# Two attention and feed-forward layers on one core: a gated unit's second product as an operation of its own, a scale moved into weights, and a newly drawn instruction order

## The chip, the cores and the metric

The kernel runs on one core of a Trainium2 chip. The metric is the device time of one execution in microseconds (us). PE is the matrix engine (TensorE; PEld is its weight loading), DVE the vector engine, ACT the scalar engine, POOL is GpSimd, and SP the queue that issues most transfers. All data are float32 except where said; a float32 product of a 128 x 512 operand shows in the trace as two matmuls.

## The reference

The input x has 128 sequences of 64 tokens with 128 features, 8192 tokens in all; the context has the same shape. Four steps follow each other, each added to x:

```python
x = x + _L0_xattn_ref(_layernorm(x), ctx, ctx, ...)   # 16 heads of 8, layer norms before and behind, gated
x = x + _L0_ffn_ref(_layernorm(x), ...)
x = x + _L1_xattn_ref(_layernorm(x), ctx, ctx, ...)   # 16 heads of 8
x = x + _L1_ffn_ref(_layernorm(x), ...)               # relu, 128 -> 512 -> 128
```

The change is in the first feed-forward. Its weights hold -1, 0 and 1, and each product is scaled by output feature:

```python
def _tlin(x, w, s):
    return jnp.einsum('bsi,oi->bso', x, w) * s
h = silu(_tlin(x, w1_w, w1_s)) * _tlin(x, w2_w, w2_s)   # 128 -> 512
h = gelu(_tlin(h, h1_w, h1_s))                          # 512 -> 512
h = gelu(_tlin(h, h2_w, h2_s))                          # 512 -> 512
return _tlin(h, w3_w, w3_s)                             # 512 -> 128
```

## The kernel before

**Tiling.** The tokens are cut into 17 chunks: one of 256 tokens, 15 of 512, one of 256 (`GROUPS`, in units of 128). Each chunk goes through four stages, each a Python generator: `attention0`, `ffn0`, `attention1`, `ffn1`. The chunk's x stays in SBUF from its load to its store. PSUM is used as eight banks of 128 x 512; a block of attention scores for four sequences takes four of them.

**The order of the work.** The kernel is written out in a fixed order by a planner that runs while the program is built (`Order`). Generators yield operations (`Op`) that name an engine, a planned length from a table (`LENGTHS`) and the buffers they take (`get`) and give back (`put`): banks, and numbered SBUF buffers such as `wk`, `hd`, `e`, `kx`, `qx`, `x` and `c`. At each step the planner takes, of all streams, the operation that can start first by its own clocks. Ties go by the stream's priority plus a small pseudo-random draw (`draw`), seeded by an entry of `DRAWS` for each 50 us of planned PE time; a seed of 0 gives no draw, and 12 of the 24 seeds are 0. Whatever the planner picks is emitted there and then, so its choice is the order of instructions on every engine. Where two engines may do an operation (`(ACT, DVE)`, `(DVE, POOL)`) the planner also picks the engine. Waits between engines are semaphores that follow from the data, not from the planned times. In the first 95 us of planned time PE's idle time is filled with small products of zeros (L428, 40 at the start, 197 in all).

**An attention stage** (`attend`, twice for a chunk of 512 tokens): scores (PE, L658) into four banks, their maximum (DVE, L662), its split in three bf16 parts ("parts", DVE or POOL, L672 to L675), the transpose of these (PE, L679; copied by ACT, L682), the scores less the maximum (PE, L691, four banks), the exponential (ACT, L696, into `e`), the weighted values (PE, L710), and small steps on ACT, DVE (L720 to L728) and POOL (L742). Layer norms take their moments on DVE (L541, L543), their inverse root on POOL (L529), and the normalising on ACT (L568) or DVE (L572); the norm behind the first attention is L564 and L876 on DVE. Transposes are L582, products for queries, keys and values L606, L618 and L631, token-major products L770.

**The first feed-forward** (`ffn0`). For each quarter k of the 512 hidden features `gated` makes two products of the normalised tokens, L903 into one bank and L904 into another, taken and given out together. ACT takes the tanh of the first (L907), and DVE makes the gated value in two steps: (tanh + 1) times the first product (L909), and that times the scales times the second product (L910). Both banks and the tanh's buffer come free behind L910. Then `square` runs twice: the 512 x 512 product in seven products of halves (PE, L956), with differences of inputs on POOL (L938), sums on DVE (L982), copies on ACT or DVE (L512, L514), and gelu on ACT (L975). At the end the token-major product with `w3` (L770) lands in a bank; DVE multiplies it by the last scale's row into a `wk` buffer (L1046), and POOL adds that to x (L1048). POOL makes the sums of weights for `square` once, early (`weights`, L896).

**Set-up on DVE.** `masks` adds up a table of head masks in five small steps (L479 to L483) and scales four biases with it (L487). `folds` folds the identity matrix into an 8-column selector in four steps (L799 to L804) and spreads it in four copies into `asel` (L808), which the scores less max use.

`ffn1` ends with the add into x (L1103) and the store (L1105). ACT changes between two function tables, one for exp and tanh and one for gelu; a load of one is ACT_TABLE_LOAD.

Of the kernel before, what the change touches and what calls it, by code (L numbers as in the profile page):

```python
# [8 lines left out]
F32 = mybir.dt.float32  # L9
# [5 lines left out]
P = 128  # L15
# [23 lines left out]
for _n, _w in _COLS:  # L39
# [25 lines left out]
DRAWS = [97, 0, 427, 0, 249, 0, 0, 0, 575, 0, 0, 112, 0, 817, 0, 39, 412, 0, 615, 329, 0, 15, 762, 0]  # L65
# [13 lines left out]
        "scores": (0.99, 0.2), "max transpose": (0.07, 0.2), "scores less max": (1.17, 0.2),  # L79
        "weighted values": (0.92, 0.2), "tokens": (0.22, 0.15), "tokens 4": (0.9, 0.15), "w12": (1.73, -0.2),  # L80
# [3 lines left out]
        "bias+": 0.28, "masks": 1.2, "gate weights": 0.4, "folds": 1.9, "moments": 1.07, "z": 1.3, "copied": 0.68,  # L84
        "scaled": 0.75, "qx": 1.5, "kx": 1.5, "vb": 1.8, "max": 2.3, "parts": 0.8, "reciprocal": 2.2, "o2": 0.83,
        "from bank": 0.68, "gate sums": 1.3, "gate": 0.4, "gained": 1.1, "gated": 1.45, "sum": 0.68, "saved": 0.68,
# [236 lines left out]
def kernel(  # L323
# [107 lines left out]
    busy(40, 7)  # L431
    ident = const.tile([P, P], F32, tag="ident", name="ident")
# [3 lines left out]
    half_mask = const.tile([P, 2, 4], F32, tag="half_mask", name="half_mask")  # L436
# [22 lines left out]
    def rowv(name, ng):  # L459
        return each(row[:, ROW[name], :], ng)  # L460
# [42 lines left out]
    fold = const.tile([P, 2, 32], F32, tag="fold", name="fold")  # L503
# [290 lines left out]
    def folds():  # L794

        yield Op(DVE, "folds")

        nc.vector.tensor_copy(identb, ident)
        nc.vector.tensor_tensor(  # L799
            fold, ident[:, 0:64].rearrange("p (r c) -> p r c", r=2), ident[:, 64:128].rearrange("p (r c) -> p r c", r=2), ALU.add  # L800
        )
        nc.vector.tensor_tensor(fold[:, 0, :], fold[:, 0, :], fold[:, 1, :], ALU.add)
        for j in range(1, 3):
            nc.vector.tensor_tensor(  # L804
                fold[:, 0, 0:8], fold[:, 0, 0:8], fold[:, 0, 8 * j : 8 * j + 8], ALU.add
            )
        for s in range(HS):
            nc.vector.tensor_copy(  # L808
                asel[:, s, :].rearrange("p (j k) -> p j k", j=2),
                fold[:, 0, 2 * s : 2 * s + 2].unsqueeze(2).to_broadcast([P, 2, 64]),  # L810
            )
# [71 lines left out]
    def weights(l):  # L883
# [131 lines left out]
    def ffn0(ci, prio):  # L1015
# [3 lines left out]
        fz = Last(fz, 4)  # L1019
# [8 lines left out]
        for l in range(2):  # L1028
# [6 lines left out]
        ps, fp, fw = yield from token_major(  # L1035
# [6 lines left out]
            own=True,  # L1042
# [5 lines left out]
        nc.gpsimd.tensor_tensor(xt, xt, y, ALU.add)  # L1048
# [148 lines left out]
```

## Time and profile before

| | us |
|---|---|
| median of 3 runs | 1130.72 (1130.66 to 1131.59) |
| the profiled execution, whole | 1129.94 |
| its span, first to last instruction | 1128.1 |
| PE busy with matmuls | 1097.8 |
| DVE busy | 865.8 |
| ACT busy | 726.2 |
| POOL busy | 504.5 |

The page gives for each engine its busy time, share of the span and number of instructions. Groups are lines of the kernel with the engine, the tiles written and read, and the mean length of one instruction in ns. A wait is the idle time of an engine ahead of an instruction, put down to the instruction that ended it. Matmul ends are modelled, so PE can be held up a little inside what is shown as busy. The granted clock is the share of its full clock that PE was given.

### The profile page before, as it was taken

The page shows a single profiled execution, that of the slowest core. Times are in us where ns is not written, and L with a number is a line of the kernel's source. Part 1 is how long each engine was busy: PE and PEld are TensorE (multiplying, and loading weights), DVE is VectorE, ACT ScalarE, POOL GpSimd, SP SyncE. Part 2 cuts the span into 40 slices and gives each one's busy share as a digit, 9 for nine tenths or more (in the row PEclk, how much of TensorE's full clock was granted, in tenths as well). Part 3 has the DMA queues.
Part 4 walks back from the last instruction along what each step waited for, and adds up shares of the span by engine and source line. Part 5 has one row for each costly group of instructions (what it writes and reads, how often), then busy time and mean ns, then how long its engine had stood idle before and what let it go on. Part 6 is the DMA issues. An engine that isn't in the chain of part 4 may idle for free.

```text
span 1128.1 us, 32895 instructions
## 1 busy us (share of the span) xinstructions
PE 1097.8 (97%) x13851; PEld 865.0 (77%) x13851; DVE 865.8 (77%) x2139; ACT 726.2 (64%) x1279; POOL 504.5 (45%) x882
## 2 busy tenths in 40 slices
PE   7799999999999999999999999999999999999998
PEld 6578687777876777878677887777778887789786
DVE  7887969888876867568878687788789888643773
ACT  5476767666776766576546686667867675545553
POOL 6744634544533445333226355335345546352221
PEclk9999999999999999999999999999999999999999
DMA  7001000000001001002100000000000000000001
GB/s 244 12 2 30 20 11 20 11 9 17 7 2 35 1 2 39 2 2 57 31 21 20 11 21 11 20 12 12 11 11 12 11 7 11 2 1 2 11 21 43
DMA packets 35444, 23.23 MB, mean 21 GB/s; under 512 B 1504, under 2 KB 34272, under 8 KB 35168
## 3 DMA queue, kind: packets, MB, share of 16 engines
q1 hardware_dynamic: 35024, 21.00, 6.2%
q8 instruction: 109, 1.79, 0.7%
q14 instruction: 39, 0.32, 0.1%
q10 hardware_dynamic: 272, 0.13, 0.0%
HBM read 16.93 MB, written 4.19 MB: 19 GB/s over the span
## 4 chain that ended last, share of the span: by engine, by line
PE 86%; DVE 10%; ACT 2%; issue 1%; POOL 1%; DMA 0%; DVEq 0%; ACTq 0%
PE banks L956 33%; PE banks L770 12%; PE banks L691 7%; PE banks L710 5%; PE banks L658 5%; PE banks L1080 5%; PE banks L903 4%; PE banks L904 4%; PE banks L582 4%; DVE m L662 3%; PE banks L631 2%; PE banks L618 2%; PE banks L606 2%; DVE su L727 1%; DVE st L541 1%
## 5 line engine op out<-in xcount | busy, mean ns | idle before, releaser
L662 DVE TENSOR_REDUCE m<-banks 128x32 f32<-128x2048 f32 x64 | 145.9, 2280 | 16.3 <-PE banks L658 15.7
L742 POOL TENSOR_TENSOR wk<-av,rec 128x256 f32<-128x256 f32 x64 | 46.8, 732 | 222.3 <-DVE rec L728 199.7
L696 ACT ACTIVATE e<-banks 128x2048 f32<-128x2048 f32 x64 | 120.2, 1878 | 36.0 <-PE banks L691 28.8
L956 PE MATMUL banks<-hd,wh 128*128 128x256 f32 (+1 forms) x544 | 127.9, 371 | 0.6 <-DVE wk L909 0.4
L956 PE MATMUL banks<-wk,wh 128*128 128x256 f32 (+1 forms) x544 | 127.5, 371 | 0.0
L956 PE MATMUL banks<-wk,ws 128*128 128x256 f32 (+1 forms) x544 | 126.2, 371 | 0.8 <-POOL wk L938 0.7
L727 DVE RECIPROCAL su<-su 128x256 f32<-128x256 f32 x64 | 111.4, 1741 | 0.0
L956 PEld LDWEIGHTS banks<-wk,wh 128*128 128x128 f32 x544 | 96.4, 190 | 18.0 <-issue 5.7
L975 ACT ACTIVATE hd<-hd,col 128x256 f32<-128x256 f32 (+1 forms) x204 | 88.8, 488 | 31.9 <-DVE hd L982 31.1
L956 PEld LDWEIGHTS banks<-hd,wh 128*128 128x128 f32 x544 | 95.4, 190 | 16.8 <-issue 4.1
L956 PEld LDWEIGHTS banks<-wk,ws 128*128 128x128 f32 x544 | 94.7, 190 | 16.5 <-issue 3.4
L982 DVE TENSOR_TENSOR hd<-banks,hd 128x512 f32<-128x512 f32 (+1 forms) x102 | 66.6, 656 | 53.0 <-PE banks L956 45.4
L529 POOL TENSOR_TENSOR nr<-nv,neg_half 128x4 f32<-128x4 f32 (+1 forms) x102 | 99.7, 977 | 8.5
L938 POOL TENSOR_TENSOR wk<-hd,wk 128x512 f32<-128x512 f32 (+1 forms) x68 | 82.4, 1212 | 40.5 <-DVE hd L910 29.0
L512 ACT COPY hd<-banks 128x512 f32<-128x512 f32 (+1 forms) x68 | 37.9, 557 | 73.0 <-PE banks L956 67.9
L568 ACT ACTIVATE wk<-x,nb,nr 128x128 f32<-128x128 f32 x192 | 79.1, 484 | 7.3 <-POOL nb L559 7.0
L658 PEld LDWEIGHTS banks<-kx,qx 32*128 32x128 f32 x2048 | 62.8, 186 | 22.4 <-issue 10.0
L710 PEld LDWEIGHTS banks<-e,vblk 128*32 128x32 f32 x4096 | 60.2, 110 | 24.0 <-issue 7.6
L658 PE MATMUL banks<-kx,qx 32*128 32x128 f32 x2048 | 74.6, 282 | 2.5 <-ACT qx L597 1.2
L710 PE MATMUL banks<-e,vblk 128*32 128x64 f32 x4096 | 70.4, 220 | 2.2 <-ACT e L696 2.2
L691 PE MATMUL banks<-qx,kx 32*128 32x128 f32 x2048 | 71.5, 277 | 0.0
L903 PE MATMUL banks<-wk,w 128*128 128x512 f32 (+1 forms) x136 | 67.7, 579 | 0.7 <-ACT wk L512 0.7
(136 smaller groups left out, 2367.8 us busy)
## 6 DMA issues: line engine op xcount, KB each, us to landing
c<-in_c_dram SPq DMA_DIRECT2D x30, 256.0 KB, 2.9
x<-in_x_dram SPq DMA_DIRECT2D x15, 256.0 KB, 3.6
out_dram<-x SPq DMA_DIRECT2D x15, 256.0 KB, 2.5
wh<-in_w_h_dram SPq DMA_DIRECT2D x1, 2048.0 KB, 12.5
c<-in_c_dram SPq DMA_DIRECT2D x4, 128.0 KB, 3.2
wa<-in_w_a_dram SPq DMA_DIRECT2D x2, 256.0 KB, 5.1
w<-in_w_dram SPq DMA_DIRECT2D x1, 512.0 KB, 7.7
wf<-in_w_f_dram SPq DMA_DIRECT2D x2, 256.0 KB, 6.9
```

What stands on the lines that cost most here:

```text
L529: nc.gpsimd.tensor_tensor(rs, ve, neg_half[:, 0:ng], ALU.pow)
L658: nc.tensor.matmul(sc[:, g, s, :], qs[h, s, :], ks[h, s, :], start=True, stop=True)
L662: nc.vector.tensor_reduce(m, sc.rearrange("p g s (j k) -> p g (s j) k", j=2), AX.X, ALU.max, negate=True,)
L691: nc.tensor.matmul(sT[:, g, s, :], lhs, rhs, start=(n == 0 and s == 0), stop=(n == 1), skip_group_check=True)
L696: nc.scalar.activation(e.rearrange("p g s i q -> p (g s i q)"), sT.rearrange("p g s c -> p (g s c)"), AF.Exp, scale=SCALE,)
L710: nc.tensor.matmul(po[32 * g : 32 * g + 32, i, s, :], vb[:, 4 * (half * HS + s) + g, i : i + 2].rearrange("p h j d -> p (h j d)"), e[:, g, ...
L727: nc.vector.reciprocal(su, su)
L770: nc.tensor.matmul(ps[:, g, :], lhs(g), w, start=(n == 0), stop=(n == len(blocks) - 1),)
L903: nc.tensor.matmul(pa, w12[:, 0, k * P : (k + 1) * P], zT, start=True, stop=True)
L938: nc.gpsimd.tensor_tensor(T[m][0], x(), y(), ALU.subtract)
L956: nc.tensor.matmul(pieces[bank][0][:, o], w[:, k, o * P : (o + 1) * P], x[:, k], start=(new and k == 0 and o == 0), stop=(k == 1), skip_gr ...
L975: nc.scalar.activation(out(i, t)[:, o], (src or out(i, t))[:, o], AF.Gelu, scale=colv(scale, 2 * i + o))
```

## The change

1. In `gated` the second product becomes an operation of its own in a stream of its own with priority 2. The planner lets it start only behind the planned end of the tanh. It takes its own bank. DVE's two steps become two operations, and the first product's bank comes free behind the first of them.
2. POOL multiplies `w3` by the last scale's row once, behind the second set of weight sums. At the end of `ffn0` DVE adds the product straight into x; the `wk` buffer, the multiplication and POOL's add go.
3. All 24 seeds of `DRAWS` are new and none is 0, so that every stretch is drawn; four planned lengths are changed and the planner's PE clock starts at 2.5 us. With 1, 2 and this, the order of instructions on every engine, and the choice of engine for operations that have two, differs from about the first microsecond on.
4. `masks` and `folds` take fewer and larger DVE steps; the last of the three blank value buffers is cleared only behind the planned landing of the hidden weights.

Cut to its core (line lengths of `DRAWS` shortened by "..."):

```diff
-DRAWS = [97, 0, 427, 0, 249, 0, 0, 0, 575, 0, 0, 112, 0, 817, ...]
+DRAWS = [45944, 71272, 38430, 71272, 71272, 71272, 71272, ...]
...
-"scores less max": (1.17, 0.2), ... "w12": (1.73, -0.2),
+"scores less max": (1.11, 0.2), ... "w12": (0.865, -0.2),
-"masks": 1.2, "folds": 1.9, ... "gated": 1.45,
+"masks": 0.9, "folds": 1.3, ... "gated a": 0.68, "gated b": 0.75,
...
     busy(40, 7)
+    order.clock[PE] = 2.5
...
     def masks():
         yield Op(DVE, "masks")
-        nc.vector.tensor_tensor(half_mask[:, 0, 0:2], hm[:, 0, 0, :], hm[:, 0, 1, :], ALU.add)
-        nc.vector.tensor_tensor(half_mask[:, 1, 0:2], hm[:, 1, 0, :], hm[:, 1, 1, :], ALU.add)
-        nc.vector.tensor_tensor(half_mask[:, 0, 2:4], hm[:, 0, :, 0], hm[:, 0, :, 1], ALU.add)
-        nc.vector.tensor_tensor(half_mask[:, 1, 2:4], hm[:, 1, :, 0], hm[:, 1, :, 1], ALU.add)
-        nc.vector.tensor_tensor(mask, half_mask[:, 0, :], half_mask[:, 1, :], ALU.add)
+        for i, order_of in ((0, "p n s t -> p t n s"), (2, "p n s t -> p s n t")):
+            nc.vector.tensor_reduce(mask[:, i : i + 2], hm.rearrange(order_of), AX.XY, ALU.add)
...
             if i < N_VB:
+                if i == N_VB - 1:
+                    yield Op(NONE, "free", after=landed[7])
                 yield Op(POOL, "blank values", put=[("vb", i)])
...
         nc.vector.tensor_copy(identb, ident)
-        nc.vector.tensor_tensor(fold, ident[:, 0:64]..., ident[:, 64:128]..., ALU.add)
-        nc.vector.tensor_tensor(fold[:, 0, :], fold[:, 0, :], fold[:, 1, :], ALU.add)
-        for j in range(1, 3):
-            nc.vector.tensor_tensor(fold[:, 0, 0:8], fold[:, 0, 0:8], fold[:, 0, 8 * j : 8 * j + 8], ALU.add)
-        for s in range(HS):
-            nc.vector.tensor_copy(asel[:, s, :]..., fold[:, 0, 2 * s : 2 * s + 2]...)
+        rows_of_8 = ident.rearrange("p (r j c) -> p c r j", j=4, c=8)[:, :, :, 0:3]
+        nc.vector.tensor_reduce(fold, rows_of_8, AX.XY, ALU.add)
+        nc.vector.tensor_copy(
+            asel.rearrange("p s (j k) -> p (s j) k", j=2), fold.unsqueeze(2).to_broadcast([P, 2 * HS, SEQ])
+        )
...
     def weights(l):
...
+        if l == 1:
+            yield Op(POOL, "weights")
+            nc.gpsimd.tensor_tensor(w3, w3, rowv("L0_ffn_w3_s", 4), ALU.mult)
...
     def gated(k, zT, n, free, d):
-        pe = yield Op(PE, "w12", get={"bank": 2, "wk": 1}, put=free)
-        pa, pb = (tile_of(s, (P, n)) for s in pe.slots["bank"])
+        got = {}
+
+        def other():
+            pe = yield Op(PE, "w12", get={"bank": 1}, put=free)
+            got["pb"] = (tile_of(pe.slots["bank"][0], (P, n)), pe.slots["bank"])
+            nc.tensor.matmul(got["pb"][0], w12[:, 1, k * P : (k + 1) * P], zT, start=True, stop=True)
+
+        pe = yield Op(PE, "w12", get={"bank": 1, "wk": 1}, put=free)
+        pa = tile_of(pe.slots["bank"][0], (P, n))
         nc.tensor.matmul(pa, w12[:, 0, k * P : (k + 1) * P], zT, start=True, stop=True)
-        nc.tensor.matmul(pb, w12[:, 1, k * P : (k + 1) * P], zT, start=True, stop=True)
         yield Op(ACT, "tanh", prio=-1)
         th = tile_of(pe.slots["wk"][0], (P, n))
         nc.scalar.activation(th, pa, AF.Tanh, scale=half_s1[:, k : k + 1])
-        yield Op(DVE, "gated", put=pe.slots["bank"] + pe.slots["wk"], prio=-1)
+        second = yield (other(), 2)
+        yield Op(DVE, "gated a", put=pe.slots["bank"], prio=-1)
         nc.vector.scalar_tensor_tensor(th, th, 1.0, pa, ALU.add, ALU.mult)
+        yield [second]
+        yield Op(DVE, "gated b", put=got["pb"][1] + pe.slots["wk"], prio=-1)
+        pb = got["pb"][0]
         nc.vector.scalar_tensor_tensor(d[k // 2][0][:, :, k % 2, :], th..., half_s12[:, k : k + 1], pb..., ALU.mult, ALU.mult)
...
     def ffn0(ci, prio):
...
-        fz = Last(fz, 4)
+        fz = Last(fz, 8)
...
-        ps, fp, fw = yield from token_major([...], ng, b[0][1] + b[1][1], own=True)
+        ps, fp = yield from token_major([...], ng, b[0][1] + b[1][1])
         yield Op(DVE, "from bank", put=fp)
-        y = tile_of(fw[0], (P, ng, D))
-        nc.vector.tensor_tensor(y, ps, rowv("L0_ffn_w3_s", ng), ALU.mult)
-        yield Op(POOL, "add", put=fw)
-        nc.gpsimd.tensor_tensor(xt, xt, y, ALU.add)
+        nc.vector.tensor_tensor(xt, ps, xt, ALU.add)
```

More of the change, by code (lines that the diff above doesn't have):

```diff
@@ L64 @@
 STRETCH = 50.0
-DRAWS = [97, 0, 427, 0, 249, 0, 0, 0, 575, 0, 0, 112, 0, 817, 0, 39, 412, 0, 615, 329, 0, 15, 762, 0]
+DRAWS = [45944, 71272, 38430, 71272, 71272, 71272, 71272, 71272, 71272, 71272, 71272, 71272, 3489, 71272, 71272, 71272, 15456, 37534, 43351, 71272, 28736, 71272, 12052, 71272]
 SPREAD = 0.1
@@ L78 @@
         "bias": (0.22, 0.25), "transpose": (0.46, 0.15), "q": (0.86, -0.2), "k": (0.94, -0.2), "v": (0.89, 0.15),
-        "scores": (0.99, 0.2), "max transpose": (0.07, 0.2), "scores less max": (1.17, 0.2),
-        "weighted values": (0.92, 0.2), "tokens": (0.22, 0.15), "tokens 4": (0.9, 0.15), "w12": (1.73, -0.2),
+        "scores": (0.99, 0.2), "max transpose": (0.07, 0.2), "scores less max": (1.11, 0.2),
+        "weighted values": (0.92, 0.2), "tokens": (0.22, 0.15), "tokens 4": (0.9, 0.15), "w12": (0.865, -0.2),
         "product": (0.865, -0.2), "f1": (0.865, -0.2),
@@ L83 @@
     DVE: {
-        "bias+": 0.28, "masks": 1.2, "gate weights": 0.4, "folds": 1.9, "moments": 1.07, "z": 1.3, "copied": 0.68,
+        "bias+": 0.28, "masks": 0.9, "gate weights": 0.4, "folds": 1.3, "moments": 1.07, "z": 1.3, "copied": 0.68,
         "scaled": 0.75, "qx": 1.5, "kx": 1.5, "vb": 1.8, "max": 2.3, "parts": 0.8, "reciprocal": 2.2, "o2": 0.83,
-        "from bank": 0.68, "gate sums": 1.3, "gate": 0.4, "gained": 1.1, "gated": 1.45, "sum": 0.68, "saved": 0.68,
+        "from bank": 0.68, "gate sums": 1.3, "gate": 0.4, "gained": 1.1, "gated a": 0.68, "gated b": 0.75, "sum": 0.68, "saved": 0.68,
         "relu": 0.7,
@@ L435 @@
     mask = const.tile([P, 4], F32, tag="mask", name="mask")
-    half_mask = const.tile([P, 2, 4], F32, tag="half_mask", name="half_mask")
     im, pm = (lambda i: mask[:, i : i + 1]), (lambda i: mask[:, 2 + i : 3 + i])
@@ L502 @@
     identb = const.tile([P, P], BF16, tag="identb", name="identb")
-    fold = const.tile([P, 2, 32], F32, tag="fold", name="fold")
+    fold = const.tile([P, 2 * HS], F32, tag="fold", name="fold")
     asel = const.tile([P, HS, P], BF16, tag="asel", name="asel")
@@ L1034, in ffn0 @@
         yield ready[0] + ready[1]
-        ps, fp, fw = yield from token_major(
+        ps, fp = yield from token_major(
             [
@@ L1041, in ffn0 @@
             b[0][1] + b[1][1],
-            own=True,
         )
         yield Op(DVE, "from bank", put=fp)
-        y = tile_of(fw[0], (P, ng, D))
-        nc.vector.tensor_tensor(y, ps, rowv("L0_ffn_w3_s", ng), ALU.mult)
-        yield Op(POOL, "add", put=fw)
-        nc.gpsimd.tensor_tensor(xt, xt, y, ALU.add)
+        nc.vector.tensor_tensor(xt, ps, xt, ALU.add)
     def context1(ci, got, prio):
```

9 lines of the change are left out of this document (removed).

## The prediction, made before the changed kernel ran

> **What bounds the kernel now.** I read the page first, then PE's idle time by stage, then who ended PE's waits, then the instructions in order of time around the longest of them.
>
> ```profile
> span 1128.1 us, 32895 instructions
> ...
> PE 1097.8 (97%) x13851; PEld 865.0 (77%) x13851; DVE 865.8 (77%) x2139; ACT 726.2 (64%) x1279; POOL 504.5 (45%) x882
> ```
>
> PE is the bound: all other engines have 23% or more to spare. None of its arithmetic goes away (both programs hold 952 hidden products, 68 first and 68 second gate products, and so on), so the change can only move PE's waits. The stages (columns: length, then busy time of PE, PEld, DVE, ACT, POOL, granted clock, DMA):
>
> ```profile
> 0.00:60.00 60.00, 44.96 (x815) 36.67 (x815) 49.34 (x156) 31.76 (x58) 40.58 (x90) 1.00 0.38 120
> 60.00:95.00 35.00, 34.11 (x408) 27.09 (x407) 28.79 (x93) 26.21 (x56) 19.19 (x31) 1.00 0.06 17
> 95.00:530.00 435.00, 429.12 (x5536) 338.02 (x5535) 340.99 (x818) 295.10 (x514) 193.25 (x334) 1.00 0.05 14
> 530.00:545.00 15.00, 12.28 (x118) 8.29 (x121) 14.65 (x36) 5.64 (x9) 5.03 (x8) 0.89 0.32 88
> 545.00:1085.00 540.00, 537.87 (x6575) 424.92 (x6568) 411.77 (x1003) 348.99 (x615) 237.24 (x401) 1.00 0.04 13
> 1085.00:1128.10 43.10, 39.43 (x415) 30.00 (x415) 20.21 (x42) 18.45 (x29) 9.24 (x18) 0.99 0.11 32
> ```
>
> Length less PE busy: 15.0 us idle in the first 60, 0.9 to 95, then 5.9, 2.7, 2.1, and 3.7 behind the last matmul. From 95 us to the end of PE's work some 10.7 us are to be had, a quarter of them in the 15 us at 530, where the clock is also lower. PE's own waits (total, times, longest):
>
> ```profile
> PE banks L679 <- DVE nmax L675: 4.0, 4, 1.4
> PE banks L770 <- DVE m L662: 2.7, 1, 2.7
> PE banks L710 <- ACT e L696: 2.2, 2, 1.1
> PE banks L770 <- ACT e L696: 2.1, 1, 2.1
> PE banks L582 <- DVE m L662: 1.6, 1, 1.6
> ```
>
> The waits for L662 are two single ones. Both stand behind the only two places where L658 runs x64 and not x32, at 49.65 and at 534.60: two score blocks, each of four banks, follow each other directly, all eight banks are full, and PE can do nothing until a maximum of 2.28 us gives four back. The second, in order of time:
>
> ```profile
> 532.84 3.23 DVE L564 SCALAR_TENSOR_TENSOR wk<-wk,mv,row 128x128 f32<-128x128 f32 x4
> ...
> 534.60 2.07 PE L658 MATMUL banks<-kx,qx 32*128 32x128 f32 x64
> ...
> 537.05 2.28 DVE L662 TENSOR_REDUCE m<-banks 128x32 f32<-128x2048 f32 x1
> ...
> 539.38 1.20 PE L770 MATMUL banks<-wa,wk 128*128 128x128 f32 x8 [2.72 <-DVE m L662]
> ...
> 540.48 3.58 PE L1080 MATMUL banks<-wk,wf 128*128 128x512 f32 x4
> ```
>
> After 2.72 us of idling, four L1080 take 3.58 us; at 345.87 four take 1.98. So this event costs 2.72 + 1.60 = 4.3 us, plus 0.14 in the eight L770 (1.20 against 1.06 at 527.06): **4.4 us**. The granted 0.89 over 15 us says the same: 0.11 x 15 = 1.65 us lost to the clock.
>
> **The change part by part**, against the profiled execution, 1129.94 us (span 1128.1 and 1.84 around it; it lies 0.8 us, 0.07%, under the median of the runs, which I do not correct for).
>
> *Order.* Almost nothing stands where it stood, so I compared both programs' orders. In the new one no two score blocks touch; at least 1.8 us of PE work lies between neighbouring blocks of four banks. So both L662 waits should go: -1.6 us at 51.7 and **-4.4 us** at 530. If another wait of that size arises, the 4.4 is given back; both ends stay in the range (0 and -6.0). For the rest I took, for each PE wait, the PE work between the matmul that feeds the releasing chain and the waiting matmul, less the mean durations of the chain's rows, queueing left out (an estimate from both orders and the rows). Before, 16 such margins are negative, the worst -1.8, -1.4, -0.9 and -0.8 us, and they are the events at 540, 539, 583 and 349. After, 30 are negative, the worst -0.8, -0.7 and -0.6, all in one place. Under 0.5 us: 97 before, 110 after. Fewer large holes, more small ones: beyond the two events I book 0, with 4 us either way.
>
> *Gated unit.* The 68 pairs of L903 and L904 were adjacent; now 3 are. PE gains no switch: between full-array lines no step costs anything, and the changes between array tilings go from 353 to 350. PE's semaphore waits go from 1227 to 1233. What is new is that the last elementwise step (L910, 716 ns) follows a matmul that comes later, and behind a late one wait the hidden products. PE work between that second matmul and the first product that reads the result is 0.9 and 1.1 us in the two tightest cases, then 2.2 or more (before 1.3, 1.6, then 2.4). Against 0.72 that is covered: 0, at worst 68 x 0.72 = 49 us if all cover went, which the order excludes. The bank of the first product comes free one L910 and one matmul sooner, a gain already inside the order.
>
> *Last scale.* Off POOL go 17 L1048 (20.6 us), on it comes one scaling of w3, 1.27 us as L896. DVE's L1046 (0.652 us) turns into an add of the same shape (L1075, 0.653): 0. PE waits for no L1048; DVE's moments did (10.1 us in 7 cases), but DVE has 23% idle. The scaling stands in POOL's queue ahead of the four small steps that feed a max transpose, early in the first feed-forward; its weights have landed by then (7.47 + 12.1 = 19.6 us). Cost 0, at most 1.3. But L1048 also slows DVE where both run:
>
> ```profile
> 759.82 3.50 DVE L564 SCALAR_TENSOR_TENSOR wk<-wk,mv,row 128x128 f32<-128x128 f32 x4
> 760.32 1.31 POOL L1048 TENSOR_TENSOR x<-x,wk 128x512 f32<-128x512 f32 x1
> ...
> 761.59 1.32 POOL L938 TENSOR_TENSOR wk<-hd,wk 128x512 f32<-128x512 f32 x1
> ...
> 764.13 0.23 PE L679 MATMUL banks<-identb,nmax 128*128 128x128 bf16 x1 [1.35 <-DVE nmax L675]
> ```
>
> Four L564 usually take 4 x 0.344 = 1.4 us (the row's median) and here 3.5, and PE waits 1.35 for what is queued behind. Of the whole row's excess, (491 - 344) x 64 = 9.4 us, some 2 us lie beside an L1048. Between 0 and -2 on PE, I take **-1.0**. The Trainium skill ("SBUF — State Buffer", Who interferes with whom) says that a DVE instruction with two SBUF inputs and a GpSimd one that reads SBUF lock each other out for a whole instruction; the row at 759.82 agrees. By the page 17 whole blocks, 20.6 us, could go. The same section speaks against the new order: it counts tensor_scalar among the operations that can take the shared ports, and DVE gets 24 more of those (next part).
>
> *Who does what.* The new order gives DVE 24 more normalising L572 (68 to 92, 432 ns mean, 338 median) and ACT 24 fewer L568, POOL 44 of 64 "parts" (40). L572's excess is (432 - 338) x 68 = 6.4 us, so 24 more bring DVE 10.4 us, 2.3 of it excess. Nothing on PE's list waits on L572: 0, range 0 to +2.3. ACT gets 85 table loads for 71: 14 x 1.283 = 18 us on an engine with 36% idle. PE's waits for e were 4.3 us with 71 loads; 14/71 of that is **+0.9**; the ends are 0 and, every load on PE's path, 18, of which the present 71 are far.
>
> *Loads and stores.* SP issues the same 79 instructions, its loads and stores drawn in a new order among themselves. After the start no engine's idle time shows a wait for an input (DVE's 3.3 us for c end at 3.31 us), and the DMA share is 0.03 to 0.05 in the long stages: 0; cover gone, one load would cost its 2.9 to 3.6 us to landing.
>
> *Start.* DVE's list of small steps shortens. L799 to L808 took 1.47 us (4.99 to 6.46); a reduce over 96 elements at 2.28/2048 us each on the 0.15 of the smallest rows is 0.25, one cast of 512 at most the 0.67 of four: 0.5 to 0.8 saved. Five mask sums took 0.61, two reduces at 0.15 take 0.3. PE's 28 fillers, which ran to 7.27 while the normalised rows were there at 6.68, are 18. PE waited 1.47 us for L591 at 11.43. So the first scores come about 1 us earlier; but the query copy now stands on ACT ahead of the next chunk's normalising, so some is lost again. **-1.0**, between -2 and +1. The second gain at 49 to 54 us (gate products stand ahead of the scores) is the -1.6 above.
>
> *End.* The last store is now 256 KB and not 128 KB: 2.5 against 2.0 us to landing, and the last add 0.69 against 0.42: **+0.8**.
>
> **Sum:** -1.0 - 1.6 - 4.4 - 1.0 + 0.9 + 0.8 = -6.3; 1129.94 - 6.3 = **1123.6 us**.
>
> By another page the event at 530 would not have been: the Trainium skill ("TensorE: Matmul & The Clock Gate", What's actually happening) lets the clock fall after an idle window of about 3.4 us, and here 2.72 sufficed. By the page only 2.7 us would go there, and the sum would be 1125.3.
>
> **Rivals.**
> 1. *More than that goes.* The margins say that the worst holes shrink everywhere, and POOL's load falls. If half of the remaining 8 us of idle and as much of the short delays go: 7 more, 1117. Against it: more margins under 0.5 us.
> 2. *Given back once.* One new wait over 2.7 us with its slow clock, +4.4, and no gain at the start, +1.0: 1129. For it: ACT's extra loads. Against it: no adjacent score blocks.
> 3. *Slower: DVE late behind POOL.* In the new order normalising and "parts" on DVE meet POOL's 1.2 us subtractions (L938), as at 485 and 760, and a maximum comes late. Each such wait costs 1.4, one over 2.7 us costs 4.4. It decides once more than two of the long kind (8.8 against the 6.3 won) arise: three give 1123.6 + 13.2 = 1136.8, two and two short ones 1135. For it: 92 L572, 110 narrow margins. Against it: 20.6 us less of POOL.
> 4. *The change does little:* waits only move from one place to another, 1131.
>
> **How the numbers follow.** Forecast 0.45, rival 1 0.17, rival 2 0.12, rival 4 0.09, rival 3 0.17. Measurement tells about 0.2% (2.3 us) from no change, so faster is 0.62, same 0.21, slower 0.17. The forecast's own terms span -3 to +4 around it (start 2, order 4, loads); the range reaches to rival 1's far side and to the near part of rival 3: 1113 to 1133.
>
> **What would show it.** No L658 x64 group; no PE wait of over 2 us after 95 us; granted clock 1.00 in every stage; PE idle from 95 to 1085 under 8 us where it was 10.7; L1048 gone and POOL near 485; ACT's table loads 85; the tail behind the last matmul some 0.8 longer. I am wrong if PE idles more than 11 us in the middle, or shows a slowed group of matmuls.

## The result, and the profile after

The changed kernel takes **1138.2 us** (median of 3 runs, 1138.02 to 1138.37) where the kernel before takes 1130.72: ratio 1.0062, 95% interval 1.0049 to 1.0076. It is slower by 0.6%. I had forecast 1123.6 in a range from 1113 to 1133, so both the sign and the range were wrong. The profiled execution took 1138.37 us, span 1136.6; the span before was 1128.1, so 8.5 us have to be found.

Lines moved a little: after's number is before's less one up to L797 and less nine from there to L887, so L563 and L571 are the normalising steps L564 and L572, L674 the last of the "parts", L827 the gate's product that was L836 and L867 the add that was L876. L904 is now the first gate product and L900 the second, L910 the first gated step and L914 the second. L942 is the subtraction that was L938, L960 the halves' product (L956), L986 its sum (L982). First the page of the changed kernel, then its stages (length, busy time of PE, PEld, DVE, ACT, POOL, granted clock, DMA):

```profile
span 1136.6 us, 32755 instructions
...
PE 1102.8 (97%) x13831; PEld 866.4 (76%) x13831; DVE 875.2 (77%) x2130; ACT 729.7 (64%) x1277; POOL 488.3 (43%) x882
```

```profile
0.00:60.00 60.00, 46.55 (x773) 38.09 (x774) 47.44 (x144) 31.28 (x65) 41.31 (x88) 0.97 0.38 120
60.00:95.00 35.00, 32.54 (x428) 25.93 (x427) 27.95 (x84) 26.53 (x53) 17.92 (x33) 1.00 0.06 17
95.00:530.00 435.00, 426.68 (x5285) 333.17 (x5284) 346.50 (x850) 286.99 (x503) 188.24 (x336) 0.99 0.05 15
530.00:545.00 15.00, 14.61 (x240) 12.22 (x239) 11.33 (x34) 11.23 (x18) 6.41 (x13) 1.00 0.13 35
545.00:1085.00 540.00, 534.95 (x6563) 420.06 (x6560) 415.99 (x965) 355.07 (x610) 227.42 (x402) 1.00 0.04 12
1085.00:1136.60 51.60, 47.45 (x574) 36.95 (x562) 26.04 (x56) 18.58 (x30) 7.03 (x13) 0.98 0.11 34
```

Length less PE busy is PE's idle time. The stage at 530 is healed as forecast: 0.4 us idle and clock 1.00, where it was 2.7 and 0.89. But 95 to 530 idles 8.3 us (5.9 before) and 545 to 1085 5.0 (2.1). The waits of PE say which:

```profile
PE banks L709 <- ACT e L695: 2.9, 3, 1.2
PE banks L678 <- DVE wk L910: 2.7, 1, 2.7
PE banks L690 <- DVE hd L986: 2.6, 1, 2.6
```

Two single waits of the size of the one that went. Both, in order of time, in the changed kernel:

```profile
255.24 1.27 POOL L942 TENSOR_TENSOR wk<-hd 128x512 f32<-128x512 f32 x1 [0.61 <-DVE hd L914]
255.28 1.37 DVE L827 SCALAR_TENSOR_TENSOR wk<-wk,gw 128x128 f32<-128x128 f32 x1
256.58 2.75 POOL L942 TENSOR_TENSOR wk<-hd,wk 128x512 f32<-128x512 f32 x2
...
256.80 1.34 DVE L827 SCALAR_TENSOR_TENSOR wk<-wk,gw 128x128 f32<-128x128 f32 x1
...
258.07 3.21 DVE L563 SCALAR_TENSOR_TENSOR wk<-wk,mv,row 128x128 f32<-128x128 f32 x4
...
262.98 0.41 PE L690 MATMUL banks<-nmT,asel 32*128 32x128 bf16 x16 [2.56 <-DVE hd L986]
...
264.26 3.68 PE L960 MATMUL banks<-hd,wh 128*128 128x256 f32 x8
```

```profile
305.25 2.71 POOL L942 TENSOR_TENSOR wk<-hd,wk 128x512 f32<-128x512 f32 x2
...
305.43 1.14 DVE L674 TENSOR_TENSOR nmax<-m,nmax 128x32 bf16<-128x32 f32 x1
...
306.50 2.05 DVE L571 TENSOR_SCALAR wk<-c,mv,nr 128x128 f32<-128x128 f32 x4
...
308.47 0.68 DVE L910 SCALAR_TENSOR_TENSOR wk<-wk,banks 128x512 f32<-128x512 f32 x1
...
309.20 0.26 PE L678 MATMUL banks<-identb,nmax 128*128 128x128 bf16 x1 [2.66 <-DVE wk L910]
309.26 2.02 PE L960 MATMUL banks<-wk,ws 128*128 128x256 f32 x4
```

Read DVE's rows against POOL's. One L827 takes 0.28 us and one that starts beside an L942 takes 1.37; four L563 take 1.4 and here 3.2; L674 takes 0.19 and here 1.14. What is queued behind them on DVE, a sum that gives banks back (L986), the first gated step that does (L910), comes late, and PE waits. So PE waits for DVE, and no PE wait stands for the result of a subtraction itself. Behind the first wait eight L960 take 3.68 us, where eight usually take 1.99 (as at 264.28 of after_again, shown further down); behind the second four take 2.02 and not 1.08. The granted clock is 0.50 for 3.41 us each time, from 264.39 and from 308.76.

Where the 8.5 us of span went (idle from the stages; "slow" is the time by which neighbouring matmuls started further apart than the tenth percentile of their line and shape, in runs where that was 1.4-fold or more):

| | us |
|---|---|
| 0 to 95, idle (15.9 both times) | 0 |
| a slow group at 31 to 36 | +1.5 |
| the event at 530: 2.3 idle, 1.5 slow | -3.8 |
| the waits at 263 and 309: 5.2 idle, 1.8 + 1.2 slow | +8.2 |
| all else from 95 to 1085 (idle -2.8 ahead of 530, +2.9 behind 545; +2.0 inside PE's busy time) | +2.1 |
| behind 1085, idle | +0.5 |

The 1.5 us at 31 to 36 are not a price of the change: before_again, the kernel before once more, has the clock at 0.50 for 6.83 us at the same place (0.94 over the first 60 us, where the profiled execution of before has 1.00), and after_again, which has no low clock there, stands level with this one at 37 us (L678 at 37.00 and 37.02), because PE then idles instead (2.46 us ahead of L678 for 0.88). What lies in the 2.1 us of "all else" stays open.

DVE's own time shows the cause in sum. I count every DVE instruction that ran over 0.3 us longer than the tenth percentile of its line and shape: before, 37 with 29.6 us in excess, 13.4 of it beside a subtraction L938; after, 41 with 36.4, **21.4 beside L942**. The L1048 took 2.0 us of the excess before and are gone.

### The profile page after: what moved, and what is told of

Same layout as the page of the kernel before. It is cut to its first block, busy times and chain, and to the rows that moved or that the text cites. A ratio compares the mean times of both kernels' runs of the same rounds, so it can differ in the third digit from the quotient of the medians.

```text
span 1136.6 us, 32755 instructions
## 1 busy us (share of the span) xinstructions
PE 1102.8 (97%) x13831; PEld 866.4 (76%) x13831; DVE 875.2 (77%) x2130; ACT 729.7 (64%) x1277; POOL 488.3 (43%) x882
## 5 line engine op out<-in xcount | busy, mean ns | idle before, releaser
L661 DVE TENSOR_REDUCE m<-banks 128x32 f32<-128x2048 f32 x64 | 146.0, 2281 | 16.2 <-PE banks L657 14.6
L960 PE MATMUL banks<-hd,wh 128*128 128x256 f32 (+1 forms) x544 | 128.5, 374 | 0.3 <-ACT kx L596 0.2
L960 PE MATMUL banks<-wk,wh 128*128 128x256 f32 (+1 forms) x544 | 128.1, 371 | 0.0
L960 PE MATMUL banks<-wk,ws 128*128 128x256 f32 (+1 forms) x544 | 124.7, 372 | 0.0
L960 PEld LDWEIGHTS banks<-hd,wh 128*128 128x128 f32 x544 | 97.3, 192 | 21.6 <-issue 7.8
L960 PEld LDWEIGHTS banks<-wk,wh 128*128 128x128 f32 x544 | 96.6, 191 | 20.9 <-issue 8.4
L960 PEld LDWEIGHTS banks<-wk,ws 128*128 128x128 f32 x544 | 96.3, 191 | 19.2 <-issue 7.3
L986 DVE TENSOR_TENSOR hd<-banks,hd 128x512 f32<-128x512 f32 (+1 forms) x102 | 66.5, 655 | 45.8 <-PE banks L960 43.7
L942 POOL TENSOR_TENSOR wk<-hd,wk 128x512 f32<-128x512 f32 (+1 forms) x68 | 82.6, 1215 | 19.8 <-PE banks L605 7.4
L567 ACT ACTIVATE wk<-x,nb,nr 128x128 f32<-128x128 f32 x176 | 72.3, 484 | 9.1 <-POOL nb L558 8.9
L690 PE MATMUL banks<-qx,kx 32*128 32x128 f32 x2048 | 71.4, 277 | 0.0
L769 PEld LDWEIGHTS banks<-wf,h 128*128 128x128 f32 x512 | 62.3, 192 | 8.9 <-issue 6.7
```

The lines of the kernel that those rows point to most:

```text
L567: nc.scalar.activation(z[:, g, :], src[:, g, :], AF.Identity, bias=nb[:, g : g + 1], scale=rs[:, g : g + 1])
L661: nc.vector.tensor_reduce(m, sc.rearrange("p g s (j k) -> p g (s j) k", j=2), AX.X, ALU.max, negate=True,)
L690: nc.tensor.matmul(sT[:, g, s, :], lhs, rhs, start=(n == 0 and s == 0), stop=(n == 1), skip_group_check=True)
L769: nc.tensor.matmul(ps[:, g, :], lhs(g), w, start=(n == 0), stop=(n == len(blocks) - 1),)
L942: nc.gpsimd.tensor_tensor(T[m][0], x(), y(), ALU.subtract)
L960: nc.tensor.matmul(pieces[bank][0][:, o], w[:, k, o * P : (o + 1) * P], x[:, k], start=(new and k == 0 and o == 0), stop=(k == 1), skip_gr ...
```

## The experiments

**Theory A**: the new order puts POOL's subtractions beside DVE instructions that they hold up, and two of these places make PE wait. **Theory B**: the split gated unit costs, through banks that L910 and L914 give back late.

**calm_two.** The changed kernel in its own order; only what six subtractions do is changed: they leave most of their arithmetic out.

```diff
+CALM = (32, 33, 34, 35, 38, 39)
...
+    differences = []
...
-            nc.gpsimd.tensor_tensor(T[m][0], x(), y(), ALU.subtract)
+            differences.append(m)
+            if CALM is None or len(differences) - 1 in CALM:
+                nc.gpsimd.memset(T[m][0], 0.0)
+                nc.gpsimd.tensor_tensor(T[m][0][:, :, 0:8], x()[:, :, 0:8], y()[:, :, 0:8], ALU.subtract)
+            else:
+                nc.gpsimd.tensor_tensor(T[m][0], x(), y(), ALU.subtract)
```

> Order of the changed kernel untouched. Six of its 136 POOL subtractions (L942), those at 255.24 to 259.29 us and at 305.25 to 306.61 us, write zeros and subtract only 8 of each 256 columns, so that part of the computation is left out. Theory A (the loss is the new order: at 262.98 and at 309.20 PE waits 2.6 us for DVE work that these subtractions hold up, and then runs slowly): both waits and the slow groups behind them go, 2.56 + 1.88 + 2.66 + 0.95 + 0.56 = 8.6 us, so 1129.6. Theory B (the split gated unit costs: the wait at 309.20 is for a bank that L910 gives back late): only the first goes, 1138.2 - 4.4 = 1133.8.

Measured: 1131.34 (one run; the kernel before on that chip 1131.54), 1.7 us above A's figure and 2.5 below B's. Its rows (lines one higher; the memset is L947, and L968 is the product L960):

```profile
255.09 0.29 DVE L828 SCALAR_TENSOR_TENSOR wk<-wk,gw 128x128 f32<-128x128 f32 x1
...
255.41 0.52 POOL L947 MEMSET wk<- 128x512 f32 x1
...
255.75 1.15 DVE L564 SCALAR_TENSOR_TENSOR wk<-wk,mv,row 128x128 f32<-128x128 f32 x4
...
260.15 0.40 PE L691 MATMUL banks<-nmT,asel 32*128 32x128 bf16 x16
```

```profile
303.35 0.22 PE L679 MATMUL banks<-identb,nmax 128*128 128x128 bf16 x1 [1.32 <-DVE wk L911]
303.40 1.08 PE L968 MATMUL banks<-wk,ws 128*128 128x256 f32 x4
```

L828 and L564 run at their usual lengths beside the memset, the wait at 263 is gone, that at 309 is half, and no slow group follows. Six POOL instructions of 136 carry 6.9 us of the 7.5: 3.9 in the two waits (2.56, and 2.66 less 1.32) and 3.0 in the low clock behind them. The run after_again below has these waits without the low clock, and took 1135.39, 4.05 more than calm_two: waits that go here are won to the end. That is A. The 1.3 us left stand behind a bank that the first gated step gives back: what B may claim here is no more than that.

**before_fold.** One part alone in the order of before: w3 scaled once on POOL, DVE adds into x, L1048 not issued.

```diff
-        y = tile_of(fw[0], (P, ng, D))
-        nc.vector.tensor_tensor(y, ps, rowv("L0_ffn_w3_s", ng), ALU.mult)
+        nc.vector.tensor_tensor(xt, ps, xt, ALU.add)
         yield Op(POOL, "add", put=fw)
-        nc.gpsimd.tensor_tensor(xt, xt, y, ALU.add)
...
+        if l == 1:
+            nc.gpsimd.tensor_tensor(w3, w3, rowv("L0_ffn_w3_s", 4), ALU.mult)
```

> Order of the kernel before, with only the last scale moved into w3 (POOL's 17 adds gone, one scaling of w3 more). Theory A: the fold helps a little where an add held up DVE, 1.35 us at 764 and little else: 1128.5 to 1130.5. If the fold itself were harmful (its scaling late in POOL's queue, or an order that leaned on the adds), 1132 or more. Theory B says nothing different.

Measured: 1131.89 (11 runs) against 1131.54, ratio 1.0004 (0.9995 to 1.0013): no change in the whole that this comparison sees, and over what I expected. At its place the edit does what I priced: the four L564 at 761 take 2.47 us where they took 3.50, and PE's wait of 1.35 behind them is 0.32. PE also keeps most of what it wins there. Both kernels run the same matmuls in the same order, so their starts can be compared one by one: the profiled execution of before_fold lies 1.8 us behind that of before ahead of this wait, 0.8 behind it (L679 starts at 764.96 and at 764.13), 0.8 still at 1040, and 1.2 at the last matmul. It was behind because of its first 61 us, where the granted clock falls to 0.50 three times (0.92 over the first 60 us, 1.00 in before). So the gain of 1.0 us is there, and the total doesn't show it: the runs of one kernel differ by more (1129.9 to 1133.5 here), and a gain of 0.6 us (0.9995) still lies in the interval.

**after_old_draws and before_new_draws.** Each kernel with the other's 24 seeds; nothing else is changed.

> The changed kernel with the 24 seeds of the kernel before: all parts but the seeds. Theory A: another order, another set of collisions; anything from 1126 to 1136, no common floor. Theory B: the split is still in, so 1134 or more.

> The kernel before with the 24 new seeds, none of the other parts. Theory A: another order again, 1126 to 1138, and its longest PE waits again behind DVE steps that POOL holds up. Theory B: no split, so 1131 or less.

Measured: 1181.62 and 1178.46. A missed both by 40 us and more, B the second by 47 (its "1134 or more" holds for the first and says little). Each set of operations under the other's seeds is some 4% slower, in waits all over: PE idles 61.8 and 56.7 us of the span where it idled 30.3, and the granted clock is 0.98 (first fence after_old_draws, second before_new_draws):

```profile
PE banks L581 <- ACT wk L567: 9.3, 2, 8.2
PE banks L709 <- ACT e L695: 7.0, 6, 3.1
PE banks L904 <- DVE m L661: 4.5, 1, 4.5
```

```profile
PE banks L956 <- DVE m L662: 4.4, 1, 4.4
PE banks L658 <- DVE m L662: 3.9, 2, 2.1
PE banks L770 <- POOL wk L742: 3.7, 1, 3.7
```

So a part of this change can't be tried alone with the order left free: the order drawn for it would move the time more than the part. All other experiments therefore keep an order as it was planned and change only what an instruction does or which engine issues it. The split can't be undone that way (the two products would need two banks at a moment when the new order grants one); **its price by itself was not tried and stays open**.

**calm_all_before and calm_all_after.** The edit of calm_two for all 136 subtractions (`CALM = None`), in each kernel's own order.

> The kernel before in its own order; all 136 subtractions L938 on POOL are replaced by a memset to zero of the tile and a subtraction over 8 of each 256 columns, so it leaves that much of the arithmetic out and POOL all but stops reading two tiles for 1.2 us at a time. Theory A (DVE held up beside POOL's subtractions, at places that the order decides): the 1.39 us wait at 486.5 goes and some of DVE's 46.6 us of slowed time, the 2.72 us wait at 536.7 stays, since it stands behind a maximum: 1128 to 1130. Rival (the subtractions' collisions are common to both orders and cost little): 1130 to 1131.5.

> The changed kernel in its own order with the same edit to all 136 subtractions L942, so the same arithmetic is left out. Theory A: the two waits of 2.56 and 2.66 us and the slowed matmuls behind them go, as in calm_two, and a little more: 1128 to 1131, level with or under the kernel before with the same edit (gap -2 to +1.5 us where it was 7.5). Rival (something else in the new order, the split gated unit or many small waits, costs the 7.5 us): 1134 or more, and a gap of 4 us or more to the kernel before with the same edit.

Measured: 1127.23 (10 runs) and 1126.61 (6 runs), against 1131.57 for the kernel before: 0.9969 (0.9952 to 0.9985) and 0.9964 (0.9952 to 0.9976). Both lie under A's ranges. The gap of 7.5 us between the medians is gone; what is left, 0.6 us, is within an error of some 2. DVE's excess falls to 15.8 and 11.8 us. But the medians hide something that the runs' mean granted clocks show. Two runs of each had a clock of 1.000: they took 1123.3 and 1123.5 us in before's order, 1126.4 and 1126.6 in the new one. So at full clock the new order is still 3 us longer, with no subtraction to blame; the split, the 110 narrow margins or anything else in the order may be in that, and nothing here separates them. The medians come out level because before's order meets the low clock more often (0.991 to 0.997 in its other eight runs, 0.997 and 0.998 in the other four of the new order).

**after_six_on_dve.** A cure that leaves nothing out: the six subtractions of calm_two go to DVE, where they stand in the program.

```diff
+ON_DVE = (32, 33, 34, 35, 38, 39)
...
+    differences = []
...
-            nc.gpsimd.tensor_tensor(T[m][0], x(), y(), ALU.subtract)
+            differences.append(m)
+            by = nc.vector if len(differences) - 1 in ON_DVE else nc.gpsimd
+            by.tensor_tensor(T[m][0], x(), y(), ALU.subtract)
```

> The changed kernel, complete, in its own order; the six subtractions L942 at 255 to 262 and at 305 to 308 us are issued on DVE and not on POOL, at the place in the program where they stand now. On DVE one should take about 0.7 us (as L910), together some 4 us more on an engine with 23% to spare. Theory A: with nothing to collide with, L827, L563, L571 and L674 run at their usual durations and both long waits go or shrink to under 1.4 us: 1131 to 1134. Rival (DVE is short of time at these two places, whoever slows it): 4 us more in its queue make the waits longer: 1138 or more.

Measured: 1131.43 (11 runs), ratio to before 1.0005 (0.9996 to 1.0013). PE's three largest sums of waits there:

```profile
PE banks L710 <- ACT e L696: 2.9, 3, 1.2
PE banks L658 <- DVE m L662: 2.2, 3, 1.5
PE banks L770 <- ACT e L696: 2.1, 1, 2.1
```

The wait at 263 is gone and that at 309 is 0.8 us, though DVE is given more to do: 0.68 us for each subtraction in place of 1.21 on POOL and some 1 us lost on DVE beside it. The rival, that DVE is short of time there whoever slows it, falls. The kernel is level with the one before and not 4 us ahead of it, as the event at 530 alone would have made it; what takes that gain away (the 2.1 us of "all else", the later end) is not shown.

**before_tuned.** The same kind of cure in the kernel before: its two subtractions at 485 on DVE, and the maximum L662 of the first of two adjacent score blocks taken in halves, so that two banks come back sooner.

```diff
+HALVED = (3, 32)
+ON_DVE = (61, 62)
...
-        nc.vector.tensor_reduce(m, sc..., AX.X, ALU.max, negate=True)
+        maxima.append(m)
+        at = HALVED is None or len(maxima) - 1 in HALVED
+        for g in ((slice(0, 2), slice(2, 4)) if at else (slice(0, 4),)):
+            nc.vector.tensor_reduce(m[:, g], sc[:, g]..., AX.X, ALU.max, negate=True)
...
-            nc.gpsimd.tensor_tensor(T[m][0], x(), y(), ALU.subtract)
+            differences.append(m)
+            by = nc.vector if len(differences) - 1 in ON_DVE else nc.gpsimd
+            by.tensor_tensor(T[m][0], x(), y(), ALU.subtract)
```

> The kernel before, complete, in its own order, with the same cure at its own two bad places: the two subtractions at 485.3 and 486.5 us go to DVE, and the maximum L662 of the first of two adjacent score blocks (at 51 and at 537 us) is taken in two halves of two banks each, so that the first two banks come back some 1.1 us sooner. Theory A with a price of 1.6 us for the slowed matmuls behind the long wait: wait at 487.9 from 1.39 to about 0.2, at 539.4 from 2.72 to about 1.5 without the slowed L1080, at 53.3 from 1.61 to about 0.5: 1125.5 to 1128.5. Rival (what is won at one place is waited for at the next): 1129.5 to 1131.

Measured: 1131.60 (11 runs), ratio 1.0000 (0.9991 to 1.0009): no gain at all, over A's range and 0.6 us over the rival's. The wait of 1.39 us at 488 is gone, but PE now waits 0.74 us at 494.8 where it waited for nothing, and the one at 540 became two (lines two to seven higher):

```profile
539.91 1.16 PE L773 MATMUL banks<-wa,wk 128*128 128x128 f32 x8 [1.65 <-DVE m L669]
541.93 0.24 PE L682 MATMUL banks<-identb,nmax 128*128 128x128 bf16 x1 [0.86 <-DVE nmax L678]
542.00 3.63 PE L1087 MATMUL banks<-wk,wf 128*128 128x512 f32 x4
```

1.65 + 0.86 for 2.72, and the slow group is still there: what the first wait gave up the second took, since the transposed maximum comes from the same DVE queue.

**after_twenty_on_dve.** The cure of after_six_on_dve for 14 more subtractions, each one beside which a DVE instruction ran long (14, 27, 43, 69, 70, 71, 77, 78, 90, 91, 102, 113, 126, 127).

> The changed kernel, complete, in its own order, with 20 of the 136 subtractions L942 on DVE: the six of after_six_on_dve and 14 more beside which a DVE instruction ran some 1 us over its usual time in that run. DVE gets 14 x 0.68 = 9.5 us more work and loses up to 14 x 1.0 us of slowed time. Theory A: calm_all_after, with no such collisions, gives the floor, 1126.6; between it and 1131.4, say 1128 to 1130.5. Rival (the six were all that PE waited for; the rest is hidden, or comes back as DVE's longer queue): 1131 to 1134.

Measured: **1128.82** (11 runs), ratio to before 0.9974 (0.9965 to 0.9983): faster than both kernels, and in A's range. DVE's excess is 16.7 us (2.3 beside subtractions). DVE is no busier for it:

```profile
PE 1102.4 (98%) x13831; PEld 867.0 (77%) x13831; DVE 867.7 (77%) x2150; ACT 730.0 (65%) x1277; POOL 465.0 (41%) x862
```

875.2 us became 867.7, though 20 instructions were added to it.

**before_fifteen_on_dve.** The same cure in before's order, for the 15 subtractions that collide there.

> The kernel before, complete, in its own order, with the same cure as after_twenty_on_dve: the 15 subtractions L938 beside which a DVE instruction ran over 0.3 us longer than usual (13.4 us of DVE's slowed time in all) go to DVE. With all subtractions reduced the two orders came within 0.6 us of each other (1127.2 and 1126.6). If the new order holds nothing else against or for it, this kernel lands within 1.5 us of after_twenty_on_dve: 1127.5 to 1130.5. If the new order, once cured, is worth what I forecast for the score blocks (4.4 us), this one stays at 1131 to 1133. If the new order is worse in something else, it falls under 1127.

Measured: 1130.57 (12 runs), ratio 0.9989 (0.9981 to 0.9998). That is 1.75 us above after_twenty_on_dve, a little outside the 1.5 that I had set for "nothing else in the new order", and 0.4 under what the 4.4 of the score blocks would have left. Cured alike, the new order is ahead by 1 to 2 us in the medians, and again by its clock: most runs of before_fifteen_on_dve have 0.994 or 0.995, where six of the eleven of after_twenty_on_dve have 0.998 or more. The one run of the former at 0.998 took 1127.31, the five of the latter 1128.33 to 1129.74. So nothing here shows that PE waits less in the new order; it keeps the full clock more often.

**before_again and after_again.** Both kernels unchanged, one more profiled execution each.

> The kernel before, unchanged, one more profiled execution. Its wait of 2.72 us at 540 should come back within 0.1 us, since it follows from the order. If the slowed matmuls behind it were its own consequence, the four L1080 take 3.58 us again; if the slow clock depends on when the execution meets some other rhythm, they take 1.9 to 3.6 and slowed groups show at other places, as in before_fold.

> The changed kernel, unchanged, one more profiled execution. The two waits of 2.56 and 2.66 us at 263 and 309 come back within 0.1 us; the slowed groups behind them (1.98 for four L960 at 264, 2.02 at 309, usually 1.1) come back if they are the waits' own consequence, and move if they are not.

Measured: 1131.10 and 1135.39. The long waits come back to 0.01 us. First before_again, then after_again:

```profile
540.51 1.55 PE L770 MATMUL banks<-wa,wk 128*128 128x128 f32 x8 [2.73 <-DVE m L662]
541.85 0.31 PE L679 MATMUL banks<-identb,nmax 128*128 128x128 bf16 x1
541.96 3.22 PE L1080 MATMUL banks<-wk,wf 128*128 128x512 f32 x4
```

```profile
263.00 0.40 PE L690 MATMUL banks<-nmT,asel 32*128 32x128 bf16 x16 [2.57 <-DVE hd L986]
...
264.28 1.99 PE L960 MATMUL banks<-hd,wh 128*128 128x256 f32 x8
...
307.54 0.22 PE L678 MATMUL banks<-identb,nmax 128*128 128x128 bf16 x1 [2.66 <-DVE wk L910]
307.59 1.08 PE L960 MATMUL banks<-wk,ws 128*128 128x256 f32 x4
```

The same eight L960 take 1.99 us where they took 3.68, the four take 1.08 for 2.02: the waits are there, the slow groups are not. At 263 both executions of the changed kernel stand level, behind the second group L690 starts at 312.07 and at 309.04, and 1138.37 - 1135.39 = 2.98 us are left at the end: that is what the two groups cost, 1.80 + 1.17. The wait belongs to the order; the low clock behind it comes in some executions only. So the change costs 4.3 us in this pair, where it cost 7.5 in the medians of the result, whose three runs all have the mean granted clock of the profiled one (0.995; after_again 0.998).

## Why the prediction was wrong, point by point

- **The failed step is the order: "beyond the two events I book 0, with 4 us either way."** My margins for each PE wait took the chains' rows at mean durations, "queueing left out". A mean spreads the collisions over all 64 instructions of a row; in the order they fall on single ones, 1 us at a time, three or four in a row (L827, L827, L563, L563 at 255 to 260), and what stands behind on DVE is late by their sum. The worst margin was -0.8 us; the waits were 2.56 and 2.66. Measured: two new long waits with the low clock behind them, +8.2 us in the profiled execution where I had 0, outside the 4 us that I allowed; 3.0 of the 8.2 are the low clock, which after_again didn't have.
- **Rival 3 named the mechanism and had the point wrong.** It had DVE late behind POOL's subtractions and "decides once more than two of the long kind arise". Two were enough. Its prices were right for that execution (4.4 forecast; 2.56 + 1.80 and 2.66 + 1.17 measured); what it was set against was not: 6.3 us of gains, of which the start's 2.6 didn't come.
- **The event at 530, -4.4:** gone as forecast, both x64 groups too; -3.8 by the stage. The same term is in part luck: 1.5 of it was the low clock, which before_fold didn't have behind the same 2.72 us (four L1080 in 1.94).
- **Start, -1.0, and the wait at 51.7, -1.6:** 0. Idle in the first 95 us is 15.9 before and after, and the first scores start at 13.20 us for 13.22: ahead of them PE waits 1.70 us for L590, where it waited 1.47 for L591. The adjacent blocks went, and the second block of scores still waits, for L661, at another place:

```profile
54.14 1.13 PE L904 MATMUL banks<-wk,w 128*128 128x256 f32 x4 [0.79 <-DVE wk L910]
...
57.66 1.17 PE L657 MATMUL banks<-kx,qx 32*128 32x128 f32 x32 [1.46 <-DVE m L661]
```

- **L1048's collision, -1.0:** true at its place, 1.0 us on PE (before_fold), too little to show in a median. The 2.0 us that DVE won beside L1048 it lost four times over beside L942.
- **L572 on DVE, 0 (to +2.3):** its excess was not the point; L571's rows beside L942 are one of the two events, so the instruction's place mattered and not its number.
- **Gated unit, 0:** not separated from the order, so open. Waits behind the first gated step name it (1.3 us in calm_two, 0.8 at 54.14), and it may be in the 3 us by which the calmed new order is longer at full clock.
- **Table loads, +0.9:** 85 as forecast, and PE's waits for e (2.9 + 2.1) are 0.7 us more than before (2.2 + 2.1): the size is right, that the loads are the reason is not shown. **End, +0.8:** 4.15 us of PE idle behind 1085 for 3.67, so +0.5.
- **The signs:** granted clock 1.00 in every stage: no (0.97, 0.99 and 0.98). PE idle from 95 to 1085 under 8 us: 13.8. "I am wrong if PE idles more than 11 us in the middle, or shows a slowed group of matmuls": both happened. No PE wait of over 2 us after 95 us: there are two. No L658 x64 group, L1048 gone, POOL at 488 and 85 table loads: as forecast.

The Trainium skill ("SBUF — State Buffer", Who interferes with whom) had spoken against the change in my own text, with 24 more instructions on DVE that can take the shared ports; I gave it 2.3 us at most. The runs agree with its rule: beside subtractions that read next to nothing DVE's excess fell from 36.4 to 11.8 us, and calm_all_after took 11.6 us off the changed kernel. What they add is how to use it: look up, in the new order, what stands beside each POOL instruction, and don't average.

## What to carry to other kernels

When an order is redrawn, walk it with the collisions in it: for each POOL elementwise instruction, see which DVE instructions start beside it, add up to a whole POOL instruction (here 1.0 to 1.1 us) for each of the kinds that the next section lists as held up, and only then compare margins. A mean over a row hides what decides. Where such a place holds up PE, giving the POOL instruction itself to DVE can cost DVE less than leaving it (0.68 us for some 1.0 lost), which is how 1138.2 became 1128.8. And before calling two orders equal by their medians, compare runs of equal granted clock.

## What the runs showed of the hardware

- **Which DVE instructions a POOL instruction holds up.** I took those that started while a POOL elementwise instruction on SBUF tiles of 256 or 512 columns was running (0.05 us behind its start, 0.15 ahead of its end at the least), and called held up what took over 0.3 us longer than the tenth percentile of its row. Held up: L564 in 11 of 14 cases before, L572 in 5 of 6, the small casts L671 and L673 in 8 of 8 after, the gate's product L827 in 8 of 12. Never: moments L541 (0 of 82), the maximum from banks L662 (0 of 14), sums from a bank and SBUF L982 (0 of 18), the gated steps (0 of 22), L727's reciprocal (0 of 10). So instructions that read a bank, moments and the reciprocal were safe neighbours here, and for the others the instant of the start decides. A memset on POOL (0.52 us) is a milder one: in calm_two it leaves L828 and L564, which read two SBUF tiles, at their lengths, and holds up the cast L674 by 0.39 us at 300.7 and an L572 by 0.37 at 301.4.
- **The low clock comes in pieces of 3.41 us, and where they lie decides.** In all fourteen executions the record of the granted clock has 1.00 or 0.50, in multiples of 3.41 us (but for the last), on a grid that lies differently in each. What a piece is given goes, as far as these traces show, by PE's busy time in the piece before. In the twelve executions in these two orders, all 17 pieces at full clock in which PE was busy for 1.45 us or less were followed by one at 0.50; of those with over 1.86 us (over 3800) none was; between 1.5 and 1.86 both occur, 9 times each. So a wait of 2.6 us that falls into one piece lowers the clock behind it, and the same wait cut in two by the grid doesn't (columns as above; two pieces of after, then two of after_again around the same wait):

```profile
260.97:264.39 3.42, 1.41 (x49) 1.29 (x49) 2.78 (x10) 1.41 (x3) 0.00 (x0) 1.00 0.00 0
264.39:267.80 3.41, 3.41 (x9) 2.69 (x10) 0.00 (x0) 3.38 (x3) 0.00 (x0) 0.50 0.00 0
```

```profile
261.71:265.12 3.41, 2.12 (x52) 1.92 (x52) 2.07 (x7) 2.12 (x3) 0.00 (x0) 1.00 0.00 0
265.12:268.53 3.41, 3.41 (x57) 2.79 (x59) 0.69 (x1) 3.37 (x4) 0.00 (x0) 1.00 0.00 0
```

  In before's order with the wait of 2.72 us at 540 five executions (before, before_again, before_fold, calm_all_before, before_fifteen_on_dve) show the low clock four times; after's two waits had it in one execution of two; and 1.65 + 0.86 us with 1.2 us of work between had it as well (before_tuned). The Trainium skill ("TensorE: Matmul & The Clock Gate", What's actually happening) has a window that runs freely, not tied to the kernel's start, which fits; its idle window of about 3.4 us does not fit pieces in which PE was busy for 1.4 us and which sufficed. Price such a group as a chance of about 1.6 us (half of 3.41 at most), not as a certainty.
- **An order drawn for one set of operations was worth 4%** here (1130.7 against 1178.5 and 1181.6 with the other kernel's seeds, one run each), six times what the change itself moved.
